# Loop one reordered: the next step's energies beside this step's transposed ones, last step's weighted values after them, then the whole products

## The chip, the cores and the metric

The kernel runs on one core of one Trainium2 chip. The metric is the time of one execution on the device in microseconds (us); less is better. Short names of the engines: PE is TensorE (matmuls), DVE is VectorE, ACT is ScalarE, POOL is GpSimd, SP issues most DMAs.

## The reference

Two layers run one after the other over `x` of 32 batches of 128 tokens by 512 features, each with a condition vector per batch. Only the first layer's loop is changed. Cut to that layer:

```python
h = gamma * layernorm(x) + beta                 # gamma, beta: one row per batch
q, k, v = split(h @ Wqkv.T + bqkv)              # 16 heads of 32 features
energy = einsum('bhqd,bhkd->bhqk', q, k)
att = softmax(energy, axis=-1) / D ** 0.5
out = einsum('bhqk,bhkd->bhqd', att, v) @ Wp.T + bp
h1 = out + x
x = gamma * layernorm(h1) + beta + h1           # same gamma, beta, weights
```

The second layer (one head, attention within a batch, a wide MLP with Gelu) follows; its kernel code is the same before and after.

## The kernel before, in words

**Loop one** is a Python loop over `STEPS` = 32 steps, unrolled. Batches are taken in groups of four (`G` = 4, eight groups); step `s` treats group `g = s // 4` and a quarter `c = s % 4` of the heads: four heads (r = 0 to 3, each 32 features, so 32 rows of the PE array) for four batches (i = 0 to 3).

The instructions of PE, DVE, ACT and POOL are issued in the order in which the code writes them (`tc.manual_schedule`); each of these queues works in that order, and waits on semaphores where data or a buffer is not ready. The order on SP is chosen by the scheduler, as are the buffers within a pool.

Parts of a step, by the names in the code:

- `qk0(s)`: two whole products (12 matmuls each, tiles `psq` and `psk`, three float32r partial products for each of four chunks); ACT adds the bias on the way out to `qk` (L548).
- `values0(b)`: one whole product of 12 matmuls (`psv`); ACT copies it out.
- `energies(s)`: q by k for four heads by four batches, with 32 rows of the array each (tiles `pse`, four banks; 32 matmul instructions); DVE takes the four maxima (`TENSOR_REDUCE`, L577) and writes `nmx`.
- `maxima(s)`: PE transposes `nmx` (`psm`). `spread_maxima(s)`: DVE spreads it into `mT` (L590).
- `exponentials(s)`: the energies transposed (`pst`, four banks), first a matmul by ones that puts in minus the maximum (L602), then k by q (L606), 32 rows each; ACT takes four exponentials (L613).
- `heads_out(s)`: the exponentials by the values (`pso`, L626) and their sums (`pss`, L631), both with 32 columns of the array for each head; ACT takes logarithm and `Exp` of its negative (L636, L637), DVE divides with three operations (L638 to L640), ACT and POOL split the result into `o..h` and `o..l`.
- `End(b)`, for a finished batch of the group before: `bias` (POOL, `xe` plus a row, L659), `stream` (the whole product `psp`, 12 matmuls), `add` (DVE, L674), `first` (statistics, DVE L688, POOL L689), `second` (DVE L693 and a store), `sums` (a load of `scw`), `third` (DVE L702).
- `Turned(layer, b)` prepares a batch: `stats`, `norm` (DVE), `halves` (ACT copy L422, then a transposing DMA), in the next step `merge` (DVE L431), `rest` (ACT) and `low` (DVE). In a step, `new` is the batch at the first half of this and `ready` the one at the second.
- `Weights.heads` and `Weights.tails`, in steps 4 to 23: ACT casts pieces of the second layer's MLP weights (`wmh`, L911), POOL subtracts (`wml`, L918) and forms sums of pieces (L921); five steps make a cycle, with one or two pieces and zero to two sums each.
- `extras`: single pieces of work in some steps (products `pswu`, `psrow`, `psc`, and `psvp` in the last four).

PSUM has eight banks: a pool `mm` of two (`mm_tile`), `s` of two (`s_tile`) and `e` of four (`e_bank`).

In step `s` the PE does, in order: `pse` of `s`, `psv`, `psq` of `s + 1`, seven matmuls of `psp`, `psm`, five more of `psp`, `pst` of `s`, `psk` of `s + 1`, `pso` and `pss` of `s`. The POOL does `rn`, End's `bias`, `re`, the add of L689, the weights' pieces and sums, and the low part of `o`. On ACT the weights' casts stand between the exponentials and the bias of `psk`.

Of the kernel before, what the change touches and what calls it, by code (L numbers as in the profile page):

```python
# [41 lines left out]
def cond_seq_kernel(ctx: ExitStack, tc, x, condT, wcond, w0, w1, wk1, wm1, wm2, cols, rows, out):  # L42
# [15 lines left out]
    def mm_tile(name):  # L58
        return ps_mm.tile([P, D], FP, tag="mm", name=name)

    def s_tile(name):
        return ps_s.tile([P, D], FP, tag="s", name=name)

    def e_bank(name):
        return ps_e.tile([P, D], FP, tag="e", name=name)
# [456 lines left out]
            row0, over_rows("psrow0", acc), ISD, bp, ALU.mult, ALU.add  # L522
        )

    def values0(b, by_part=False):
        g, i = divmod(b, G)
        hT = hs[0, g][0]

        def done(ps):
            if i == 0:  # L530
                vs[g] = w_tile(f"v{g}", FP)
            nc.scalar.copy(vs[g][:, i], ps)

        return mm3(
            lambda: mm_tile(f"psv{b}"),
            [(sub(hT, k, ts(i, P)), sub(W0["v"], k)) for k in range(KC)],
            done, by_part,
        )
# [54 lines left out]
        )  # L593
        mT[s] = t.rearrange("p i q -> p (i q)")

    def exponentials(s):

        banks = [e_bank(f"pst{s}_{r}") for r in range(4)]
        q, k = qk[s][:, 0], qk[s][:, 1]
        for r in range(4):  # L600
            rr = slice(32 * r, 32 * r + 32)
            nc.tensor.matmul(banks[r], over[rr], mT[s][rr], start=True, stop=False)  # L602
        for i in range(G):
            for r in range(4):
                rr = slice(32 * r, 32 * r + 32)
                nc.tensor.matmul(  # L606
                    banks[r][:, ts(i, P)], k[rr, ts(i, P)], q[rr, ts(i, P)],
                    start=False, stop=(i == G - 1),
                )
        es[s] = []  # L610
        for r in range(4):
            e = p_tile(f"e{s}_{r}")
            nc.scalar.activation(e, banks[r], AF.Exp)  # L613
            es[s].append(e)

    def heads_out(s):

        g, c = divmod(s, KC)
        e, v = es.pop(s), vs[g]
        if c == 0:  # L620
            os_[g] = w_pair(f"o{g}")
        pso, pss = s_tile(f"pso{s}"), s_tile(f"pss{s}")
        for i in range(G):
            for r in range(4):
                rr = slice(32 * r, 32 * r + 32)
                nc.tensor.matmul(  # L626
                    pso[rr, ts(i, P)], v[:, i, 32 * (4 * c + r) : 32 * (4 * c + r) + 32],
                    e[r][:, ts(i, P)], start=True, stop=True,
                )
        for r in range(4):  # L630
            nc.tensor.matmul(  # L631
                pss[32 * r : 32 * r + 32], rootd, e[r], start=True, stop=True
            )

        w = p_tile(f"rs{s}")
        nc.scalar.activation(w, pss, AF.Ln)  # L636
        nc.scalar.activation(w, w, AF.Exp, scale=-1.0)  # L637
        nc.vector.tensor_tensor(pss, pss, w, ALU.mult)  # L638
        nc.vector.tensor_tensor(w, pso, w, ALU.mult)
        nc.vector.scalar_tensor_tensor(w, pss, 2.0, w, ALU.subtract, ALU.mult, reverse0=True)  # L640
        hi, lo = (t[:, c] for t in os_[g])
        nc.scalar.copy(hi, w)
        nc.gpsimd.tensor_tensor(lo, w, hi.bitcast(FP), ALU.subtract)

    class End:
# [15 lines left out]
        def stream(self):  # L661
            g, i = divmod(self.b, G)

            def done(ps):
                self.ps = ps

            return mm3(
                lambda: mm_tile(f"psp{self.b}"),
                [(sub(os_[g], k, ts(i, P)), sub(W0["p"], k)) for k in range(KC)],
                done,  # L670
            )
# [516 lines left out]
    with tc.manual_schedule(engines=ordered):  # L1188
# [67 lines left out]
        for p in first:  # L1256
            p.stats()
            p.norm()
        run(values0(0, True))
        energies(0)  # L1260
        run(values0(1))
        first[0].rest()
        new = Turned(0, G + 2)
        new.stats()
        run(values0(2))
        cond_rows()
        maxima(0)
        spread_maxima(0)
        new.norm()
        new.halves()  # L1270
        run(values0(3))
        W0["p"] = w_pair("w0p")
        ready = first[1]

        def l1_chunk(j, c):
            return load(d_tile(f"w1c{j}_{c}", FP, (P, KC, P)), w1[:, j, :, ts(c, P)])
# [30 lines left out]

        def coming(s):

            if s + G + 2 < B:  # L1310
                return Turned(0, s + G + 2)
            return Turned(1, s - FIRST1) if s >= FIRST1 else None

        CQ = range(7, 15, 2)
        W_FIRST, W_STEPS = 4, len(Weights.TURNS)
        end = past = None
        staged = None
        for s in range(STEPS):
            q, k = qk0(s + 1) if s + 1 < STEPS else ([], [])
            if s:  # L1320
                energies(s)
            else:
                ready.rest()
                ready = None
            if ready:
                ready.merge()
            if 0 < s <= B - G:
                run(values0(s - 1 + G))
            if s >= STEPS - KC:
                staged()  # L1330
                staged = None
            run(q)
            projection = end.stream() if end else []

            ahead = 5 if s == STEPS - 1 else 7
            run(projection[:ahead])
            if s:
                maxima(s)
            if 0 < s < KC or s == STEPS - 1:
                spread_maxima(s)  # L1340
            if ready:
                ready.rest()
            if new and s:
                new.stats()
            if KC <= s < STEPS - 1:
                spread_maxima(s)
            if ready and s == STEPS - 1:
                ready.low(nc.vector)
            if new and s:
                new.norm()  # L1350
            if end:
                end.bias()
            if ready and s < STEPS - 1:
                ready.low()
            if end:
                run(projection[ahead:])
                end.add()
                end.first()
            elif staged:
                staged()  # L1360
                staged = None
            wn, wj = divmod(s - W_FIRST, W_STEPS)
            if s == KC:
                cond_features()
            if new and s:
                new.halves()
            exponentials(s)
            q2, late = divmod(s - W_FIRST, 3)
            if not late and 0 <= q2 < 4:
                nc.scalar.dma_start(out=w2d[q2], in_=wm2[:, q2])  # L1370
            if 0 <= wn < KC:
                weights.heads(wj)
                weights.tails(wj)
            if past:
                past.third()
                past = None
            if "cq" in L1:
                L1.pop("cq")()
            if end:
                end.second()  # L1380
                past = end
            if s == 0:
                staged = extras[0]()
            if s < KC:
                split_w(W0["p"], raw["p"], s, nc.gpsimd)
            coming_stage = extras[s + 1]() if s + 1 in extras else None
            run(k)
            if s == STEPS - 1:
                K = keys1(0)
                run(K[0])  # L1390
            heads_out(s)
            ready, new = new, coming(s + 1) if s + 1 < STEPS else None
            end = End(s + 1 - G, s + 1 == STEPS) if s + 1 >= G else None
            if past:
                past.sums()
            if s in CQ:
                L1["cq"] = l1_cq(CQ.index(s))
            if staged:
                staged()
            staged = coming_stage  # L1400
            if s == 2:
                later["mods"] = r_tile("mods")
            wn, wj = divmod(s + 1 - W_FIRST, W_STEPS)
            if 0 <= wn < KC and wj == 0:
                weights = Weights(wn)
            if s == STEPS - 2:
                l1_load()

        ends = [end]
        begins = {2 * b - 22: lambda b=b: Turned(1, b) for b in range(2 * G, B)}
        for b, slot in ((G + 1, -11), (G + 2, -10), (G + 3, -8)):
            begins[slot] = lambda b=b: Turned(1, b)
# [5 lines left out]
        for u, stream in enumerate(products):  # L1420
            pipe.start(u - 11)
            if u == 1:
                ready.merge()
            if isinstance(stream, int):
                e = ends[stream]
                e.bias()
                run(e.stream())
                e.add()
                e.put_off()
                if stream + 1 < G:  # L1430
                    ends.append(End((NG - 1) * G + stream + 1, True))
            else:
                run(stream)
            if u == 1:
                ready.rest()
                past.third()
            if u == 2:
                ready.low()
            pipe.end(u - 11)
# [153 lines left out]
```

## Time and profile before

| | before |
| --- | --- |
| time, median of 3 runs | 1455.6 us (1455.53 to 1456.17) |
| the profiled execution: its own time | 1455.66 us |
| its span | 1453.9 us, 24645 instructions |
| PE busy | 1441.2 us (99%) |
| DVE busy | 1032.8 us (71%) |
| ACT busy | 758.7 us (52%) |
| POOL busy | 434.9 us (30%) |
| chain that ended last, by engine | PE 88%, DVE 6%, ACT 2%, DMA 2%, POOL 1% |
| granted PE clock | 1.0 |

The span is one execution seen by the profiler; the profiled execution's own time is 1.8 us longer. A line of a timeline gives start and duration in us, engine, line of the kernel, operation, output and inputs, shapes and how many instructions are merged in it. Matmuls overlap in the pipeline, so the distance between starts tells more than a duration. Where an engine was idle before an instruction, the idle time and its releaser stand in brackets. Loop one's first `pse` starts at 34.9 us, and the first product after the loop's last heads starts at 553.5 us.

### The profile page before, as it was taken

The page shows a single profiled execution, that of the slowest core. Times are in us where ns is not written, and L with a number is a line of the kernel's source. Part 1 is how long each engine was busy: PE and PEld are TensorE (multiplying, and loading weights), DVE is VectorE, ACT ScalarE, POOL GpSimd, SP SyncE. Part 2 cuts the span into 40 slices and gives each one's busy share as a digit, 9 for nine tenths or more (in the row PEclk, how much of TensorE's full clock was granted, in tenths as well). Part 3 has the DMA queues.
Part 4 walks back from the last instruction along what each step waited for, and adds up shares of the span by engine and source line. Part 5 has one row for each costly group of instructions (what it writes and reads, how often), then busy time and mean ns, then how long its engine had stood idle before and what let it go on. Part 6 is the DMA issues. An engine that isn't in the chain of part 4 may idle for free.

```text
span 1453.9 us, 24645 instructions
## 1 busy us (share of the span) xinstructions
PE 1441.2 (99%) x9224; PEld 1142.8 (79%) x9224; DVE 1032.8 (71%) x1906; ACT 758.7 (52%) x1392; POOL 434.9 (30%) x396
## 2 busy tenths in 40 slices
PE   9999999999999999999999999999999999999998
PEld 5777777777777667887888888888888888888887
DVE  6668898988888788889987866755566655753442
ACT  4556656655665455677786454534453444523231
POOL 0125555464552334556560313100020002210000
PEclk9999999999999999999999999999999999999999
DMA  8446677947565355777798976846784676834450
GB/s 326 125 141 190 196 231 185 246 141 212 158 201 150 101 174 148 186 209 204 202 218 297 305 228 203 313 152 193 232 278 163 209 230 208 297 130 159 168 181 29
DMA packets 227871, 287.80 MB, mean 198 GB/s; under 512 B 107396, under 2 KB 138244, under 8 KB 226216
## 3 DMA queue, kind: packets, MB, share of 16 engines
q1 hardware_dynamic: 218240, 226.89, 52.6%
q10 hardware_dynamic: 9512, 59.34, 12.1%
q8 instruction: 72, 1.18, 0.3%
q14 instruction: 47, 0.39, 0.1%
HBM read 193.18 MB, written 73.60 MB: 183 GB/s over the span
## 4 chain that ended last, share of the span: by engine, by line
PE 88%; DVE 6%; ACT 2%; DMA 2%; POOL 1%; issue 1%; SPq 0%; POOLq 0%; ACTq 0%; DVEq 0%
PE acc L1044 24%; PE psh L164 21%; PE psp L164 6%; PE psk L164 6%; PE psv L164 5%; PE psq L164 5%; PE psT L164 4%; PE psV L164 4%; PE pso L626 2%; PE pse L565 2%; PE pss L631 2%; PE pst L606 2%; PE pss L809 1%; PE pso L164 1%; PE pst L602 1%; DVE nm L577 1%
## 5 line engine op out<-in xcount | busy, mean ns | idle before, releaser
L337 POOL TENSOR_TENSOR rn<-vn,neghalf 128x1 f32<-128x1 f32 x96 | 60.0, 625 | 510.2 <-DVE vn L335 372.8
L422 ACT COPY tn<-x 128x1024 uint16<-128x1024 uint16 x90 | 94.1, 1046 | 75.4 <-DVE x L408 61.1
L982 ACT ACTIVATE c<-c,col 128x512 f32<-128x512 f32 x64 | 46.4, 725 | 141.4 <-DVE c L1007 88.0
L1060 POOL TENSOR_TENSOR xe<-xe,row 128x512 f32<-128x512 f32 x32 | 45.2, 1443 | 202.3 <-DMA xe<-xs 156.4
L997 DVE TENSOR_TENSOR c<-psh,ca 128x512 f32<-128x512 f32 x32 | 22.1, 691 | 87.0 <-PE psh L164 83.4
L431 DVE COPY tn<-tn 128x1024 uint16<-128x1024 uint16 x90 | 79.1, 879 | 0.4 <-DMA tn<-tn 0.4
L577 DVE TENSOR_REDUCE nm<-pse 128x4 f32<-128x512 f32 x128 | 79.2, 681 | 0.0
L613 ACT ACTIVATE e<-pst 128x512 f32<-128x512 f32 x128 | 65.8, 600 | 1.8 <-PE pst L606 1.8
L325 DVE BATCH_NORM_STATS2 stn<-x 128x6 f32<-128x512 f32 x96 | 65.4, 681 | 1.9 <-DMA x<-in_x 1.8
L693 DVE SCALAR_TENSOR_TENSOR xe<-te,re,xe 128x512 f32<-128x512 f32 x28 | 40.9, 1462 | 28.6 <-POOL xe L689 28.6
L408 DVE TENSOR_SCALAR x<-x,rn 128x512 f32<-128x512 f32 x64 | 56.6, 884 | 6.2 <-POOL rn L337 5.4
L448 ACT ACTIVATE tn<-tn,mods 128x128 f32<-128x128 f32 x128 | 52.6, 483 | 14.0 <-DVE tn L431 14.0
L548 ACT ACTIVATE qk<-psq,col 128x512 f32<-128x512 f32 x32 | 22.1, 690 | 63.6 <-PE psq L164 62.6
L337 POOL TENSOR_TENSOR re<-ve,neghalf 128x1 f32<-128x1 f32 x32 | 30.8, 963 | 75.4 <-DVE ve L330 72.6
L565 PEld LDWEIGHTS pse<-qk 32*128 32x128 f32 x1024 | 32.0, 186 | 26.7 <-issue 18.4
L1010 DVE TENSOR_TENSOR ca<-psh,ca 128x512 f32<-128x512 f32 x32 | 22.1, 691 | 42.4 <-PE psh L164 42.4
L982 ACT ACTIVATE cb<-cb,col 128x512 f32<-128x512 f32 x32 | 23.2, 726 | 41.6 <-DVE cb L1011 41.6
L659 POOL TENSOR_TENSOR xe<-xe,row 128x512 f32<-128x512 f32 x32 | 42.2, 1317 | 2.3 <-DMA xe<-in_x 2.3
L638 DVE TENSOR_TENSOR pss<-pss,rs 128x512 f32<-128x512 f32 x32 | 22.3, 697 | 28.9 <-ACT rs L637 28.7
L448 ACT ACTIVATE tn<-tn,mod 128x128 f32<-128x128 f32 x104 | 42.6, 482 | 0.2 <-DVE tn L431 0.2
L1064 DVE TENSOR_TENSOR xe<-acc,xe 128x512 f32<-128x512 f32 x32 | 21.1, 688 | 30.3 <-PE acc L1044 30.3
L918 POOL TENSOR_TENSOR wml<-wm,wmh 128x512 fp32r<-128x512 f32 x28 | 40.8, 1468 | 0.0
(1388 smaller groups left out, 4741.7 us busy)
## 6 DMA issues: line engine op xcount, KB each, us to landing
mod<-mod SPq DMA_DIRECT2D x32, 512.0 KB, 5.9
x<-xs SPq DMA_DIRECT2D x64, 256.0 KB, 4.0
ur<-ud SPq DMA_DIRECT2D x64, 256.0 KB, 4.7
xs<-xe SPq DMA_DIRECT2D x60, 256.0 KB, 2.7
xe<-xs SPq DMA_DIRECT2D x60, 256.0 KB, 3.3
x<-in_x SPq DMA_DIRECT2D x32, 256.0 KB, 4.0
xe<-in_x SPq DMA_DIRECT2D x32, 256.0 KB, 3.9
scw<-scw SPq DMA_DIRECT2D x32, 256.0 KB, 4.9
```

Source lines behind the costliest of these rows:

```text
L164: nc.tensor.matmul(st["ps"], *calls[j], start=(j == 0), stop=(j == n - 1))
L325: nc.vector.bn_stats(st, t)
L337: nc.gpsimd.tensor_tensor(r, v, neghalf, ALU.pow)
L408: nc.vector.tensor_scalar(X, X, r, None, ALU.mult)
L422: nc.scalar.copy(halves.rearrange("p (e d) -> p e d", e=2), X.bitcast(U16).rearrange("p (d e) -> p e d", e=2),)
L431: nc.vector.tensor_copy(self.a.bitcast(U16).rearrange("p (f e) -> p e f", e=2), self.t.bitcast(U16).rearrange("p (e f) -> p e f", e=2),)
L448: nc.scalar.activation(dst[:, c], self.a[:, ts(c, P)], AF.Identity, bias=m[:, q + B : q + B + 1], scale=m[:, q : q + 1],)
L565: nc.tensor.matmul(banks[r][:, ts(i, P)], q[32 * r : 32 * r + 32, ts(i, P)], k[32 * r : 32 * r + 32, ts(i, P)], start=True, stop=True,)
L577: nc.vector.tensor_reduce(nm[:, r], chunks(banks[r]), AX.X, ALU.max, negate=True)
L613: nc.scalar.activation(e, banks[r], AF.Exp)
L982: nc.scalar.activation(t[nm], t[nm], AF.Gelu, bias=col[:, C_B1 + f : C_B1 + f + 1], scale=1.0)
L1044: nc.tensor.matmul(accs[i], u[pa][:, ts(i, P)], wb[f // 4][pb][:, f % 4, :], start=(first and j == 0), stop=(last and j == len(PARTS) - 1),)
```

## The change

The step is put in another order. Step `s` now begins with the energies of step `s + 1`, then the transposed energies of step `s` (`scores0`, split off from `exponentials`), then `heads_out` of step `s - 1`; after these come the whole products `psv`, (`psm` of `s + 1`), `psq` and `psk` of step `s + 2`, and `psp`, now in one piece. The three divisions and the split of the output are split off into `divided0`. `End.bias`, `stream` and `add` stand at the step's end, `first`, `sums`, `second` and `third` in the next step; an `End` object, and so its loads, is made within the step. The weights' casts stand after the bias of `psk` and after `halves`, and the weights' pieces and sums before `End.bias`. Batches are prepared one step earlier. What ran ahead of the loop now takes in `qk0(1)`; the last `heads_out` and division stand behind the loop.

The PSUM banks are dealt out anew: `pst` in two `mm` and two `s` banks (before four `e`), `pso` and `pss` in `e` (before `s`), `psv` in `e` (before `mm`), `psp` in `s` (before `mm`).

```diff
-    def exponentials(s):
+    def scores0(s):
-        banks = [e_bank(f"pst{s}_{r}") for r in range(4)]
+        banks = [(mm_tile if r < 2 else s_tile)(f"pst{s}_{r}") for r in range(4)]
...
-        es[s] = []
+        es[s] = banks
+
+    def exponentials(s):
+
         for r in range(4):
             e = p_tile(f"e{s}_{r}")
-            nc.scalar.activation(e, banks[r], AF.Exp)
-            es[s].append(e)
+            nc.scalar.activation(e, es[s][r], AF.Exp)
+            es[s][r] = e
...
-        pso, pss = s_tile(f"pso{s}"), s_tile(f"pss{s}")
+        pso, pss = e_bank(f"pso{s}"), e_bank(f"pss{s}")
...
+        es[s] = pso, pss, w
+
+    def divided0(s):
+
+        g, c = divmod(s, KC)
+        pso, pss, w = es.pop(s)
...
-                lambda: mm_tile(f"psp{self.b}"),
+                lambda: s_tile(f"psp{self.b}"),
```

The loop's body after the change, with the core of it in order:

```python
last = s == STEPS - 1
if not last:
    energies(s + 1)
scores0(s)
if s:
    heads_out(s - 1)
if ready:
    ready.merge()
exponentials(s)
if past:
    past.first()
    past.sums()
if s:
    divided0(s - 1)
if 0 < s <= B - G:
    run(values0(s - 1 + G))
if s >= STEPS - KC:
    staged()
    staged = None
if not last:
    maxima(s + 1)
if ready:
    ready.rest()
if last:
    ready.low(nc.vector)
if new:
    new.stats()
if not last:
    spread_maxima(s + 1)
end = End(s - G) if s >= G else None
q, k = qk0(s + 2) if s + 2 < STEPS else ([], [])
run(q)
if past:
    past.second()
if new:
    new.norm()
if ready and not last:
    ready.low()
run(k)
if s == KC:
    cond_features()
if new:
    new.halves()
...
if 0 <= wn < KC:
    weights.heads(wj)
    weights.tails(wj)
if past:
    past.third()
...
if end:
    end.bias()
    run(end.stream())
    end.add()
past = end
...
ready, new = new, None if last else coming(s + 1)
...
if staged:
    staged()
```

More of the change, by code (lines that the diff above doesn't have):

```diff
@@ L523, in l0_row, with values0 @@
         )
-    def values0(b, by_part=False):
+    def values0(b, by_part=False, make=None):
         g, i = divmod(b, G)
@@ L534, in values0 @@
         return mm3(
-            lambda: mm_tile(f"psv{b}"),
+            lambda: (make or e_bank)(f"psv{b}"),
             [(sub(hT, k, ts(i, P)), sub(W0["v"], k)) for k in range(KC)],
@@ L1258, in cond_seq_kernel @@
             p.norm()
-        run(values0(0, True))
+        run(values0(0, True, mm_tile))
         energies(0)
-        run(values0(1))
+        run(values0(1, make=mm_tile))
         first[0].rest()
@@ L1264, in cond_seq_kernel @@
         new.stats()
-        run(values0(2))
+        run(values0(2, make=mm_tile))
         cond_rows()
@@ L1270, in cond_seq_kernel @@
         new.halves()
-        run(values0(3))
+        q, k = qk0(1)
+        run(q)
+        first[1].rest()
+        run(k)
+        run(values0(3, make=mm_tile))
         W0["p"] = w_pair("w0p")
-        ready = first[1]
         def l1_chunk(j, c):
@@ L1308, in coming @@
         def coming(s):
-            if s + G + 2 < B:
-                return Turned(0, s + G + 2)
+            if s + G + 3 < B:
+                return Turned(0, s + G + 3)
             return Turned(1, s - FIRST1) if s >= FIRST1 else None
@@ L1315, in cond_seq_kernel @@
         W_FIRST, W_STEPS = 4, len(Weights.TURNS)
-        end = past = None
+        ready, new, end, past = new, coming(0), None, None
         staged = None
         for s in range(STEPS):
-            q, k = qk0(s + 1) if s + 1 < STEPS else ([], [])
+            last = s == STEPS - 1
+            if not last:
+                energies(s + 1)
+            scores0(s)
             if s:
[L1321 to L1324, printed above, removed]
+                heads_out(s - 1)
             if ready:
                 ready.merge()
+            exponentials(s)
+            if past:
+                past.first()
+                past.sums()
+            if s:
+                divided0(s - 1)
             if 0 < s <= B - G:
@@ L1331, in cond_seq_kernel @@
                 staged = None
[L1332 to L1340, printed above, removed]
+            if not last:
+                maxima(s + 1)
             if ready:
                 ready.rest()
-            if new and s:
+            if last:
+                ready.low(nc.vector)
+            if new:
                 new.stats()
[L1345 to L1349, printed above, removed]
+            if not last:
+                spread_maxima(s + 1)
+            end = End(s - G) if s >= G else None
+            q, k = qk0(s + 2) if s + 2 < STEPS else ([], [])
+            run(q)
+            if past:
+                past.second()
+            if new:
                 new.norm()
-            if end:
-                end.bias()
-            if ready and s < STEPS - 1:
+            if ready and not last:
                 ready.low()
[L1355 to L1362, printed above, removed]
+            run(k)
             if s == KC:
                 cond_features()
-            if new and s:
+            if new:
                 new.halves()
-            exponentials(s)
             q2, late = divmod(s - W_FIRST, 3)
@@ L1370, in cond_seq_kernel @@
                 nc.scalar.dma_start(out=w2d[q2], in_=wm2[:, q2])
+            wn, wj = divmod(s - W_FIRST, W_STEPS)
             if 0 <= wn < KC:
@@ L1375, in cond_seq_kernel @@
                 past.third()
-                past = None
             if "cq" in L1:
                 L1.pop("cq")()
-            if end:
-                end.second()
-                past = end
             if s == 0:
@@ L1386, in cond_seq_kernel @@
             coming_stage = extras[s + 1]() if s + 1 in extras else None
-            run(k)
-            if s == STEPS - 1:
+            if end:
+                end.bias()
+                run(end.stream())
+                end.add()
+            past = end
+            if last:
                 K = keys1(0)
                 run(K[0])
[L1391 to L1395, printed above, removed]
+            ready, new = new, None if last else coming(s + 1)
             if s in CQ:
@@ L1407, in cond_seq_kernel @@
                 l1_load()
-        ends = [end]
+        heads_out(STEPS - 1)
+        past.first()
+        past.sums()
+        divided0(STEPS - 1)
+        ends = [End((NG - 1) * G, True)]
         begins = {2 * b - 22: lambda b=b: Turned(1, b) for b in range(2 * G, B)}
@@ L1433, in cond_seq_kernel @@
                 run(stream)
+            if u == 0:
+                past.second()
             if u == 1:
```

## The prediction

> **What bounds the kernel now.** I read the page's busy line first, then the timeline of TensorE over one step of loop one (the 32 steps stand between 35 and 553 us), then the timelines of the other engines over the same step, and the order of the changed program's instructions with their waits.
>
> ```profile
> PE 1441.2 (99%) x9224; PEld 1142.8 (79%) x9224; DVE 1032.8 (71%) x1906; ACT 758.7 (52%) x1392; POOL 434.9 (30%) x396
> ```
>
> TensorE is the bound. In its timeline (start, duration, line, tile) one step reads:
>
> ```profile
> 302.05 0.40 PE L164 MATMUL psp<-w0ph,o3l 128*128 128x512 f32 x1
> ...
> 302.38 0.51 PE L602 MATMUL pst<-mT,over 32*128 32x512 f32 x4
> 302.71 1.06 PE L606 MATMUL pst<-qk 32*128 32x128 f32 x32
> 303.70 0.50 PE L164 MATMUL psk<-n_16h,w0kh 128*128 128x512 f32 x1
> 304.04 0.40 PE L164 MATMUL psk<-n_16l,w0kh 128*128 128x512 f32 x1
> ...
> 306.33 0.39 PE L164 MATMUL psk<-n_16h,w0kl 128*128 128x512 f32 x1
> 306.64 1.08 PE L626 MATMUL pso<-e,v 128*32 128x128 f32 x32
> 307.54 1.04 PE L631 MATMUL pss<-e,rootd 128*32 128x512 f32 x8
> 308.51 1.17 PE L565 MATMUL pse<-qk 32*128 32x128 f32 x32
> 309.62 0.50 PE L164 MATMUL psv<-w0vh,n_20h 128*128 128x512 f32 x1
> 309.95 0.39 PE L164 MATMUL psv<-w0vl,n_20h 128*128 128x512 f32 x1
> ```
>
> Whole matmuls start every 0.227 us; sets of four row-tiled ones every 0.112, column-tiled every 0.109. Wherever the tile shape changes, the next block starts about 0.1 late and its first set takes about 0.1 longer, its weight load standing bare. Step by step the energies (pse) of this kernel start exactly 15.79 us apart from step 5 to 26, with no other gap: nothing but matmuls and five changes of shape.
>
> The other engines in that step:
>
> ```profile
> 303.48 0.68 DVE L674 TENSOR_TENSOR xe<-psp,xe 128x512 f32<-128x512 f32 x1
> ...
> 312.01 2.48 DVE L577 TENSOR_REDUCE nm<-pse 128x4 f32<-128x512 f32 x4
> ```
>
> ```profile
> 302.99 1.05 ACT L422 COPY tn<-x 128x1024 uint16<-128x1024 uint16 x1 [0.50 <-DVE x L410]
> ...
> 305.87 0.64 ACT L911 CAST wmh<-wm 128x512 fp32r<-128x512 f32 x1
> 306.75 0.69 ACT L548 ACTIVATE qk<-psk,col 128x512 f32<-128x512 f32 x1 [0.24 <-PE psk L164]
> ```
>
> ```profile
> 301.38 1.29 POOL L659 TENSOR_TENSOR xe<-xe,row 128x512 f32<-128x512 f32 x1
> ...
> 307.66 1.26 POOL L918 TENSOR_TENSOR wml<-wm,wmh 128x512 fp32r<-128x512 f32 x1
> 308.89 3.11 POOL L921 TENSOR_TENSOR wm<-wm 128x512 f32<-128x512 f32 x2
> ```
>
> The reader is to see an order: End.bias (L659) runs on POOL before the weights' casts, and so the add (L674) follows psp at once; wmh is cast before k's bias.
>
> **What is saved.** By the single starts, a change into row tiles costs 0.21, out of them to whole 0.20 to 0.22, whole to column 0.115, column to row 0.21: 0.95 a step. The new step has row tiles (pse of s+1, then pst of s), column tiles, whole: three changes. Whole to row is 0.21; column to whole is not in the trace and lies between 0.20 and 0.22, its neighbours; row to column lies between 0.115 and 0.21, and I take 0.13, since the exposed load is the column one's (0.02). Work 14.77, changes 0.55, slow first spacings 0.04: 15.36 instead of 15.79, or 0.43 saved a step (0.35 with the dear end).
>
> **What is moved past what.** In the changed program POOL's order is: rn, the weights' lows (wml), their sums, and only then End.bias; ScalarE's order is k's bias, halves (L422), then wmh. So bias now stands at the end of a chain that starts with the last psk matmul. VectorE's add waits for bias. Behind the add stand the four maximum reductions, merge and everything else of the next step on VectorE; and the order with waits shows that the ones-matmul of pst bank 3 of the next step waits for that add, because psp now uses that bank (s_tile). TensorE is in order, so it stops there.
>
> Measured from the start K of the last psk matmul: k's bias starts at K+0.42 (306.33 to 306.75), the next ScalarE operation 0.60 later (q's bias and its follower: 299.62 to 300.21), after halves another 0.95 (302.99 to the exponentials at 303.94), the cast takes 0.64, the hand-over 0.05: the first wml starts at K+2.66. Each wml occupies POOL 1.24 (307.66 to 308.89). A sum takes 1.29 where VectorE is quiet and up to 1.74 beside its work (its own rows); VectorE is waiting here, so I take 1.27 apart. Then bias 1.29, add 0.68, two hand-overs: bias start plus 2.06. Without the wait the bank-3 matmul would start at K+0.23+2.72 (psp)+0.10+1.00 (pse) = K+4.04.
>
> The weights' work runs in steps 4 to 23 as a cycle of five, four times over: pieces (wml) and sums 2+0, 1+1, 1+2, 2+1, 1+0. Bank 3 is ready at K+7.20, 7.23, 8.50, 8.47, 5.96; stalls 3.16, 3.19, 4.46, 4.43, 1.92: 17.2 a cycle, 68.6 in all. With sums at 1.74 it is 76; below, the least rows give 67. Nothing hides it: the four reductions, merge, the exponentials and the divisions of the next step need the add or these matmuls first.
>
> SP: the load of xe is now issued in mid-step, but behind the preceding step's last wml store, some 14 us before bias needs it, against 3.9 us to land; mod (5.9 us), scw (4.9 us) and the transposes (3.2 us) land before their readers too. I cost them at nothing; if one fell late by 1 us in weights steps the same wait would cover it.
>
> The other steps, 24 to 27, gain 0.43 each. There bias follows rn directly and is done some 3 us before psp ends. The other new waits have little room: the add frees bank 3 about 0.15 before its use, and the first maximum frees pso's bank 0.34 before (energies' end, 0.68 of reduction), the third the values' bank 1 us before. Cost nothing, at worst half a microsecond a step.
>
> Start: step 0 has neither heads nor values between scores and maxima, so the transposed maxima wait for 2.8 us of reductions: 1.8 lost. The wu product at the step's end waits for VectorE's column sums, 0.9, and these hold the next reductions, 0.5; after cond_half(1), now last in step 3, five VectorE operations (3.5) stand before the reductions, 2.1. Together 5.3. Before had 1.9 of stalls there (0.97 in values after wu, 0.8 in pso, 0.15), and three and a half steps' changes save 1.5: net +1.9.
>
> End: in steps 29 to 31 psvp directly follows heads (no values left) and takes the bank that the first exponential frees; ScalarE does logarithm and reciprocal first, so TensorE waits pss end + 1.8 to 2. Before lost 0.5 there: with the saving +1.05 in 29 and 30. Step 28 gains 0.43; step 31 I count as even (no energies, but K of loop two late).
>
> **The sum**, against the profiled execution's 1455.66 (span 1453.9; the median of three runs is 1455.6, the same): steps 4 to 23 -8.6 +68.6, 24 to 28 -2.1, 29 to 31 +2.1, start +1.9: +62, or 1517.6.
>
> [...] The windows view at the kernel's end shows TensorE's last work (to 1449.97) and the granted clock:
>
> ```profile
> 1449.00:1450.00 1.00, 0.97 (x5) 0.47 (x3) 1.00 (x2) 0.00 (x0) 0.00 (x0) 1.00 0.38 145
> ...
> 1453.00:1454.00 1.00, 0.00 (x0) 0.00 (x0) 0.00 (x0) 0.00 (x0) 0.00 (x0) 0.73 0.00 0
> ```
>
> The clock falls to half at 1453.46, 3.5 us after. The first warm matmuls (256 columns) stand 0.427 apart, as far as 512 columns do from 6.3 us on: half speed for some 4.7 us of work. Idle stretches of 4.2 us come in eight steps of my sum; if each drops the clock for 4.7 us, TensorE loses 2.35 each, 19 in all; if none does, 0. I take 0, since one fall after 3.5 does not say that 4.2 suffices wherever it lies.
>
> [...]
>
> **Rivals.** *Late bias and the clock falls* in the eight long stalls: up to 1537. [...] *Late bias, but the changes of shape save nothing* (the load stays bare, another gap replaces it): 25 steps at 0.43 back, 1528. Against it: the gaps are the same in every step. *Faster:* bias is in time. Its place is POOL between rn and wml, the price of the stall is 0, and the rest leaves -6.7: 1449. It decides at K+2.95, psp's end: bias must be done by then. Since wmh is cast only after k's bias and halves, the first wml alone starts at K+2.66; only a POOL that does not work in order, or weights' steps that read little, would give that. The timelines show POOL in order.
>
> **Chances.** Late bias as summed 0.79, with the clock 0.10, without saving 0.05, faster 0.05, near no change 0.01. The likeliest is 1517.6. The range 1503 to 1537 takes in the terms' ends (stalls 67 to 76, start and end a few us either way, the hand-overs) and the clock case, and leaves out the faster one. What can be told from no change is 0.2%, 2.9 us: faster 0.05, same 0.01, slower 0.94.
>
> **What would show it.** Right: in steps 4 to 23 pse starts 17 to 20 us apart in a cycle of five, TensorE idle before L602's fourth matmul with VectorE's add as releaser, the add waiting for POOL's bias, and 15.36 in steps 24 to 27 with no gap between pse and pst. Wrong: steps of 15.4 throughout, bias done before psp's end, or waits that sit at pso (the maxima) or at psm instead.

## The result and the profile after

| | before | after |
| --- | --- | --- |
| time, median of 4 runs each | 1455.6 us (1455.0 to 1456.2) | 1565.8 us (1562.4 to 1567.6) |
| ratio to before, 95% interval | | 1.0754 [1.0733, 1.0776] |
| span of the profiled execution | 1453.9 us | 1565.4 us |
| mean granted clock of the span | 1.0 | 0.971 |
| first product after the loop's last heads | 553.5 us | 665.0 us |

The change costs 110 us, and in the traces all of it lies in loop one: the first product behind the loop starts 111.5 us later, the span is 111.5 us longer.

The page of the changed kernel: TensorE's busy line, the clock over forty slices of the span, and two groups (busy time and mean ns of one, then the idle time before them and who ended most of it).

```profile
PE 1476.4 (94%) x9224; PEld 1172.8 (75%) x9224; DVE 1009.4 (64%) x1906; ACT 753.6 (48%) x1392; POOL 429.2 (27%) x396
...
PEclk9999999899998999899999999999999999999999
...
L683 DVE TENSOR_TENSOR xe<-psp,xe 128x512 f32<-128x512 f32 x32 | 22.1, 690 | 128.1 <-POOL xe L668 120.7
...
L602 PE MATMUL pst<-mT,over 32*128 32x512 f32 x128 | 28.6, 492 | 67.0 <-DVE xe L683 66.0
```

The same 9224 matmuls fill 94% of a longer span, and they take 35 us longer in sum. The add (L683, 674 before) waits for POOL's bias (L668), and the ones-matmul L602 for the add. The list of TensorE's waits between 120 and 530 us has one line (total, times, longest):

```profile
PE pst L602 <- DVE xe L683: 62.2, 20, 4.7
```

One pause for each of the twenty steps with weights' work. The timeline of one of them:

```profile
473.96 0.69 ACT L548 ACTIVATE qk<-psk,col 128x512 f32<-128x512 f32 x1 [1.05 <-PE psk L164]
474.54 1.04 ACT L422 COPY tn<-x 128x1024 uint16<-128x1024 uint16 x1
475.48 0.62 ACT L920 CAST wmh<-wm 128x512 fp32r<-128x512 f32 x1
...
476.18 1.27 POOL L927 TENSOR_TENSOR wml<-wm,wmh 128x512 fp32r<-128x512 f32 x1 [4.22 <-ACT wmh L920]
...
477.41 2.60 POOL L930 TENSOR_TENSOR wm<-wm 128x512 f32<-128x512 f32 x2
477.48 0.49 PE L602 MATMUL pst<-mT,over 32*128 32x512 f32 x3
...
479.97 1.26 POOL L668 TENSOR_TENSOR xe<-xe,row 128x512 f32<-128x512 f32 x1
481.26 0.69 DVE L683 TENSOR_TENSOR xe<-psp,xe 128x512 f32<-128x512 f32 x1 [7.51 <-POOL xe L668]
...
482.01 0.79 PE L602 MATMUL pst<-mT,over 32*128 32x512 f32 x1 [4.04 <-DVE xe L683]
```

Read it downwards: k's bias, halves, cast, one piece, two sums, bias, add, and only then the fourth ones-matmul. Each line starts where the one before it ends; this is one chain over four engines. What the forecast left out stands in the windows view of the same place (length, then busy time and instructions of PE, PEld, DVE, ACT, POOL, then the granted clock):

```profile
477.90:481.30 3.40, 0.07 (x3) 0.00 (x0) 0.04 (x1) 0.00 (x0) 3.25 (x3) 1.00 0.99 275
481.30:484.70 3.40, 2.69 (x41) 2.45 (x45) 3.33 (x8) 0.00 (x0) 0.00 (x0) 0.55 0.12 45
484.70:488.10 3.40, 3.40 (x41) 1.62 (x33) 1.63 (x5) 0.00 (x0) 0.55 (x1) 0.50 0.02 5
```

After the pause the clock is at half for 6.8 us. In it sets of four matmuls of pso start 0.213 us apart (0.109 at full clock), whole matmuls 0.427 (0.227). Over loop one the records show 26 such stretches of 3.41 us, 88.8 us at half clock; TensorE was busy in 84.5 of them, so at about half speed it loses some 42. Twenty of the stretches stand behind 15 of the twenty pauses, one at the loop's start and five in its last three steps.

### The profile page after: what moved, and what is told of

It reads as the page before. It is cut to its first block, busy times and chain, and to the rows that moved or that the text cites. A ratio compares the mean times of both kernels' runs of the same rounds, so it can differ in the third digit from the quotient of the medians.

```text
span 1565.4 us, 24861 instructions
## 1 busy us (share of the span) xinstructions
PE 1476.4 (94%) x9224; PEld 1172.8 (75%) x9224; DVE 1009.4 (64%) x1906; ACT 753.6 (48%) x1392; POOL 429.2 (27%) x396
## 4 chain that ended last, share of the span: by engine, by line
PE 75%; DVE 8%; POOL 6%; issue 5%; ACT 3%; DMA 2%; SPq 0%; POOLq 0%; DVEq 0%; ACTq 0%
PE acc L1053 22%; PE psh L164 19%; PE psT L164 5%; PE psv L164 4%; PE psq L164 4%; PE psk L164 3%; PE psV L164 3%; PE pso L629 3%; PE pst L606 2%; POOL wml L927 2%; PE pss L634 2%; PE psp L164 2%; POOL xe L668 1%; POOL wm L930 1%; PE psvp L757 1%
## 5 line engine op out<-in xcount | busy, mean ns | idle before, releaser
L337 POOL TENSOR_TENSOR rn<-vn,neghalf 128x1 f32<-128x1 f32 x96 | 69.6, 725 | 449.9 <-DVE vn L335 367.8
L639 ACT ACTIVATE rs<-pss 128x512 f32<-128x512 f32 x32 | 19.2, 599 | 249.6 <-PE pss L634 249.6
L683 DVE TENSOR_TENSOR xe<-psp,xe 128x512 f32<-128x512 f32 x32 | 22.1, 690 | 128.1 <-POOL xe L668 120.7
L1069 POOL TENSOR_TENSOR xe<-xe,row 128x512 f32<-128x512 f32 x32 | 45.3, 1444 | 202.1 <-DMA xe<-xs 183.3
L602 PE MATMUL pst<-mT,over 32*128 32x512 f32 x128 | 28.6, 492 | 67.0 <-DVE xe L683 66.0
L431 DVE COPY tn<-tn 128x1024 uint16<-128x1024 uint16 x90 | 78.4, 871 | 11.2 <-DMA tn<-tn 8.8
L337 POOL TENSOR_TENSOR re<-ve,neghalf 128x1 f32<-128x1 f32 x32 | 24.1, 752 | 173.7 <-DVE ve L330 168.4
L602 PEld LDWEIGHTS pst<-mT,over 32*128 32x128 f32 x128 | 11.2, 190 | 74.3 <-DVE xe L683 72.6
L606 PE MATMUL pst<-qk 32*128 32x128 f32 x1024 | 52.0, 322 | 0.0
L629 PE MATMUL pso<-e,v 128*32 128x128 f32 x1024 | 47.7, 345 | 2.9 <-DVE nm L577 2.9
L606 PEld LDWEIGHTS pst<-qk 32*128 32x128 f32 x1024 | 46.7, 225 | 0.2
```

Source lines behind the costliest of these rows:

```text
L337: nc.gpsimd.tensor_tensor(r, v, neghalf, ALU.pow)
L431: nc.vector.tensor_copy(self.a.bitcast(U16).rearrange("p (f e) -> p e f", e=2), self.t.bitcast(U16).rearrange("p (e f) -> p e f", e=2),)
L606: nc.tensor.matmul(banks[r][:, ts(i, P)], k[rr, ts(i, P)], q[rr, ts(i, P)], start=False, stop=(i == G - 1),)
L629: nc.tensor.matmul(pso[rr, ts(i, P)], v[:, i, 32 * (4 * c + r) : 32 * (4 * c + r) + 32], e[r][:, ts(i, P)], start=True, stop=True,)
```

## The experiments

Theory: the late bias makes the pauses, and the pauses make the half clock. Rivals: the new order itself slows TensorE; or the clock falls for some other reason than idle time.

**1. The bias early.** One step of the code is moved:

```diff
             wn, wj = divmod(s - W_FIRST, W_STEPS)
+            if end:
+                end.bias()
             if 0 <= wn < KC:
                 weights.heads(wj)
                 weights.tails(wj)
...
             if end:
-                end.bias()
                 run(end.stream())
```

> The changed kernel with one edit: End.bias (POOL) stands before the weights' casts, pieces and sums instead of after them. Late-bias theory (the add waits for bias, bank 3 of the transposed energies waits for the add, and the idle stretches make the clock fall): in steps 4 to 23 pse starts 15.4 us apart as in steps 25 and 26 of the changed kernel (15.35), no half clock between 130 and 510 us, the time 1565.8 - 62 (waits there) - 36 (slow clock there) - 3, so 1455 to 1470, of which about 10 are lost in steps 0 and 29 to 31. Rival, the new deal of the PSUM banks (psp in an s bank, the add frees it too late whenever bias is done): the waits of L602 for the add stay above 1 us a step, the time stays over 1500.

Measured: 1475.7 us, ratio 1.0137 [1.0114, 1.016], mean clock 0.988. TensorE's waits between 120 and 530 us:

```profile
PE pst L602 <- DVE xe L683: 4.8, 3, 2.9
PE pse L565 <- DVE x L410: 2.7, 2, 2.2
PE psvp L757 <- ACT e L616: 1.9, 1, 1.9
```

Of 62.2 us 4.8 are left; 90 of the 110 us come back by the place of one POOL instruction. Most distances between energies are now 15.35 (I number them: the nth goes from `pse` of n to `pse` of n + 1 and holds loop step n - 1; the expectations from here on count steps so, but for the loop's last ones). The time is still some 6 us above what I expected: numbers 9 to 16 hold one of 20.4 and one of 21.5 us and lose about 15 in all, taken up in 6 to 8. (Each stands behind a transposing DMA that went out at once, 0.03 us after `halves`, but took 7.8 and 8.8 us to land, against a median of 4.2.)

**2. The casts before the keys instead.** `weights.heads` and `weights.tails` in front of `run(k)`, the bias left at the end.

> The changed kernel with the weights' casts, pieces and sums moved before the product k and its bias on ScalarE; End.bias stays behind them on POOL. Late-bias theory: the chain to the add begins one product (2.7 us) and halves (0.95) earlier, so steps with 2+0, 1+1 and 1+0 pieces and sums have no wait, those with 1+2 and 2+1 about 0.8 us; no long idle stretch, no slow clock in steps 5 to 24; time 1465 to 1478. Rival (bias waits for something else, such as the load of xe, or VectorE is late by itself): waits as before the edit, time over 1540.

Measured: 1534.2 us, ratio 1.0539 [1.0505, 1.0573]. A miss by some 60 us. TensorE's and VectorE's waits in the same stretch:

```profile
PE pst L602 <- DVE xe L683: 31.2, 16, 3.5
PE pse L565 <- ACT qk L548: 9.0, 4, 3.3
```

```profile
DVE tn L431 <- DMA tn<-tn: 30.9, 13, 5.1
```

Half of the old wait is left, and a new one has come. The timeline of SP at one of these steps:

```profile
301.34 0.49 SPq L934 DMA_DIRECT2D ad<-wml  x1
301.93 4.11 SPq L426 DMA_TRANSPOSE tn<-tn  x1
```

The transposing DMA now comes behind the store of wml, which I had not counted, but that is the smaller part: `halves` ends at 301.60, so it goes out 0.33 us later here and 1.0 in the median (0.03 in the changed kernel). It also takes longer to land, a median of 6.2 us instead of 3.1; why, no run separates. The merge (L431) of the next step waits for it (5.1 us at most), and VectorE's divisions, ScalarE's splits and casts and then k's bias, which the next energies need, are late behind it.

**3. The pauses filled.** Useless matmuls in each pause, into banks that the real ones overwrite:

```diff
+        for _ in range((11, 11, 17, 17, 6)[s % 5] if 5 <= s <= 24 else 0):
+            for r in range(3):
+                rr = slice(32 * r, 32 * r + 32)
+                nc.tensor.matmul(banks[r], over[rr], mT[s][rr], start=True, stop=True)
         for r in range(4):
```

> The changed kernel with useless matmuls by ones into banks 0 to 2 of the transposed energies ahead of the real ones, in steps 5 to 24: 6, 11 or 17 sets of three, sized to fill most of the wait for bank 3 (1.4 to 3.9 us); their results are overwritten. Theory that the half clock after idle stretches costs 36 us there: the chain through POOL is as long as before, the clock stays full in steps 5 to 24, and the kernel is faster with more work: 1526 to 1534. Rival (the steps over 17 to 18.5 us come from longer POOL or ScalarE work, not from the clock): no gain, 1560 to 1575.

Measured: 1537.1 us, ratio 1.056 [1.0528, 1.0591]: more work, and 28.6 us faster than the changed kernel. The windows view from 130 to 235 us, of the changed kernel and then of this one:

```profile
130.00:235.00 105.00, 87.70 (x804) 67.03 (x808) 62.45 (x125) 46.98 (x87) 42.24 (x38) 0.92 0.59 164
```

```profile
130.00:235.00 105.00, 103.41 (x1096) 80.43 (x1091) 68.33 (x138) 50.34 (x94) 47.34 (x40) 1.00 0.61 173
```

The fourth ones-matmul still starts only when the add has ended, and the clock does not fall here. In the twenty filled steps it falls once, at 326.2 us, behind 2.8 us of a longer pause that the fill left open (number 16, 22.9 us). So the half clock comes from idle time and not from the order or from load. The other steps, now free of it, measure the pauses: 18.6, 18.8, 20.0, 19.85, 17.3 us (one of 17.75), that is 3.3, 3.4, 4.6, 4.5 and 2.0 above 15.35. The forecast had 3.16, 3.19, 4.46, 4.43, 1.92.

**4. Only the sums behind the bias.** `Weights.tails` split in two: the pieces stay where they are, the sums follow `end.bias()`.

> The changed kernel with only the sums of the weights' pieces (0, 1, 2, 1, 0 in the five steps of a cycle) moved behind End.bias on POOL; the pieces stay ahead of it. Late-bias theory: waits fall by 1.27 us for each sum, to 3.2, 1.9, 1.9, 3.2, 1.9 us by the cycle, 12.1 instead of 17.2: 20 us less waiting, and the clock falls in fewer steps; 1525 to 1545. Rival (only the first cast counts, the queue behind it does not): no change, 1560 to 1570.

Measured: 1527.5 us, ratio 1.0493 [1.0462, 1.0524], TensorE's wait 41.9 us. Steps with one piece take 17.3 to 17.4 whatever sums they have, steps with two pieces 20.15 to 20.2, of which 1.7 is for a half-clock stretch (number 16: 23.05). What POOL does ahead of the bias is paid for nearly in full, as the sum had it.

**5. The pauses half filled.** As 3, with `(5, 5, 8, 8, 3)`.

> The changed kernel with useless matmuls in about half of each pause of TensorE in steps 5 to 24 (they write banks that the real ones then overwrite); the waits stay as they are and the idle time that is left in a pause is 1.0 to 2.1 us instead of 1.9 to 4.5. Theory that the clock falls after a 3.41 us stretch of the grid in which TensorE worked less than about half: nearly all of the 34 us come back, 1531 to 1541 (a few stretches with 2.1 us idle still fall). Rival, that any pause of over 1 us is followed by a stretch at half clock: 1555 to 1566. Rival, that only a wholly idle stretch of 3.41 us counts: the clock is full in all of steps 5 to 24, 1530 to 1533; but then the pauses of under 3.2 us in the changed kernel should not have cost anything either.

Measured: 1560.4 us, ratio 1.0728 [1.0707, 1.075]. My theory's number missed: the steps with the longer pauses take 20.25 to 22.9 as without fill, but for 18.75 and 19.9 in numbers 17 and 18 (number 16: 23.5). What is left of the pauses, 1.6 to 2.2 us (3.5 in number 16), still drops the clock except in these two; the shortest pauses, 0.8 us, don't. The windows view on the grid of 3.413 us on which the clock changes in the changed kernel's trace (see the last section), here:

```profile
189.71:193.12 3.41, 1.92 (x27) 1.24 (x21) 0.13 (x1) 0.00 (x0) 3.25 (x3) 1.00 1.17 166
193.12:196.53 3.41, 2.79 (x41) 2.55 (x45) 3.34 (x8) 0.00 (x0) 0.00 (x0) 0.50 1.13 358
```

and in the changed kernel, around a pause of 2.9 us that a boundary of the grid cuts into 1.3 and 1.5:

```profile
355.32:358.73 3.41, 2.09 (x39) 1.38 (x37) 0.00 (x0) 0.22 (x1) 2.98 (x3) 1.00 0.72 157
358.73:362.15 3.42, 1.87 (x53) 1.75 (x57) 2.62 (x5) 0.00 (x0) 0.77 (x1) 1.00 0.71 231
362.15:365.56 3.41, 3.41 (x37) 2.23 (x30) 3.27 (x9) 1.87 (x4) 0.81 (x1) 1.00 0.15 52
```

and there again, around a pause of 2.8 us that lies within one stretch:

```profile
437.24:440.66 3.42, 0.66 (x15) 0.45 (x16) 1.19 (x2) 0.00 (x0) 2.19 (x2) 1.00 0.97 252
440.66:444.07 3.41, 3.41 (x66) 3.05 (x62) 3.34 (x8) 0.00 (x0) 0.00 (x0) 0.50 0.76 231
```

In the half-filled run 1.5 us idle in one stretch brought half clock. In the changed kernel 2.8 us in one stretch did, and 2.9 us across a boundary cost nothing. The time lies where the first rival had it, but its rule does not hold either, since the pause of 2.9 us and pauses of 1.5 us in the changed kernel cost nothing; and the second rival falls, for no wholly idle stretch is needed. What decides in these traces is how much of one stretch is idle. About half is the border and not a sharp one: with 1.92 us busy the clock fell, with 1.87 it did not.

**6 to 8. What was left with the early bias.** I put the 15 us of numbers 9 to 16 down to `l1_cq`, which in steps 7, 9, 11 and 13 loads two rows through SP. First they were moved (`CQ = range(22, 26)`):

> The bias early, as in the run before it (1475.7 us), and the four pieces of layer one's query row (l1_cq, two small loads each at the end of a step) moved from steps 7, 9, 11, 13 to steps 22 to 25. Theory: in steps 8 to 16 of the run with the early bias about 15 us were lost (steps of 20.4 and 21.5 us among steps of 15.35) because those loads wait on SyncE's queue for a buffer (up to 7.1 us) and the next load of x and the transposing DMA stand behind them, so that GpSimd's rn (5.2 us) and VectorE's merge (4.5 us) come late. Then the steps go to 15.35 and the time to 1460 to 1464; the steps 23 to 26, which have little work on GpSimd, lose under 3 us. Rival: the loss comes from the weights' stores in those steps; then the time stays at 1474 to 1478.

Measured: 1471.3 us, ratio 1.0116 [1.0096, 1.0136]. Distances 6 to 14 go to 15.35, about 2 us stay in 15 and 16, but 25 to 28 lose 9: the trouble moves with the loads, and the time misses the 1460 to 1464 expected. With three more waits mended:

> As the run with the early bias and the later query row, and three more waits of the changed kernel taken away: the value weights of layer one in steps 29 to 31 in a bank of the energies' pool instead of one that waits for the first exponential (1.9 us each), the VectorE row of step 4 that follows the conditioning's second half (2.9 us) put into the middle of the step, and VectorE's weighted sum behind the addition in the last two steps (3.8 us). Theory: 3 + 3 x 1.9 + 3.8 us and the half clock that follows them, some 3.5 us: 1445 to 1452, faster than the kernel before (1455.6). Rival: another wait in steps 29 to 31 comes last in their place: 1455 to 1462.

Measured: 1467.1 us, ratio 1.0083 [1.0061, 1.0106]. Number 30 fell from 19.7 to 16.0, but VectorE's row, moved into the middle of step 4, gained 3 us in number 5 and lost 6.4 in 6 and 7. A miss. Then the loads on ScalarE's queue, in their old steps, to see whether it is SP's order:

> As the run with the early bias, and: the two loads of layer one's query row stay in steps 7, 9, 11, 13 but go out on ScalarE's queue, which runs behind the work that frees their buffers, instead of SyncE's; the value weights of layer one in steps 29 to 31 in a bank that doesn't wait for the first exponential; the conditioning's second half ahead of the keys of step 3; VectorE's weighted sum behind the addition in the last two steps. Theory: the 15 us of steps 9 to 16 come back (the queue is what holds the merges), 3.7 us in step 29, 2 to 3 us in step 4, some 4 us in steps 30 and 31: 1475.7 less 20 to 25, so 1451 to 1456. Rival: ScalarE's queue holds the halves instead (0.4 to 0.8 us of issue in front of the keys' bias), or the merges wait still: 1460 to 1472.

Measured: 1473.5 us, ratio 1.0132 [1.0112, 1.0152]: numbers 9 to 16 still lose 20 us. The theory of the queue falls: between 130 and 430 us the transposing DMAs go out 0.03 us after `halves`, so nothing on SP holds them, but two land only 8.1 and 11.6 us later, and the merges wait. Two of SP's waits between 160 and 310 us in this run:

```profile
SPq L86 <- POOL o2l L652: 13.9, 2, 8.3
SPq L86 <- POOL o3l L652: 9.0, 1, 9.0
```

Its loads (L86) wait, with the rows gone from SP, for POOL's last read of a buffer of the pool of eight that exponentials, divisions and rows share. In runs 6 and 7, with the rows in later steps, SP has no such wait there. So two more buffers taken in a step look like the cost, whoever issues the loads; how that makes the transfers land late is not shown. The companion run, with the rows late and the queries of step 0 moved up:

> As the run before it, but the query row's loads on SyncE's queue and in steps 22 to 25, as in the run that moved them, where steps 25 to 28 then lost 9 us; and the queries of step 0 ahead of its maxima (a wait of 1.9 us and the half clock after it). Theory: 1471.3 less 3.7, 2 to 3, 4 and 2: 1457 to 1461. Rival: step 0 waits for the first exponential instead, and nothing comes back there: 1460 to 1464.

Measured: 1463.0 us, ratio 1.0063 [1.0048, 1.0078]; loop step 0 lost 3 us instead of gaining (15.4 instead of 12.4; `pswu` waited 4.6 us for VectorE), and the time lies where the rival had it, for another reason than the rival's.

**9 and 10. A version that beats both.** The rows in a tile of another pool, and the end of the loop rearranged:

```diff
-        w, bq = load(p_tile(f"wk{c}"), wk1[:, c]), row_of(R_BQ1)
+        w, bq = load(w_tile("wq", FP), wk1), row_of(R_BQ1, make=l_tile)
...
-        banks = [(mm_tile if r < 2 else s_tile)(f"pst{s}_{r}") for r in range(4)]
+        pools = [mm_tile, mm_tile, s_tile, e_bank if s == STEPS - 1 else s_tile]
+        banks = [pools[r](f"pst{s}_{r}") for r in range(4)]
...
+            if s == STEPS - 2:
+                maxima(s + 1)
+                spread_maxima(s + 1)
             if past:
                 past.first()
```

> All that helped so far in one kernel: the bias early; layer one's query row from one tile of another pool, loaded in step 23 and used in steps 24 to 27, so that no step takes two more of the eight buffers that the exponentials share; the value weights of layer one not behind the first exponential; the conditioning's second half ahead of the keys of step 3; and for the last two steps the maxima of step 31 ahead of the other work of VectorE in step 30, the next piece of weights loaded earlier, and the last bank of step 31's transposed energies from the energies' pool, so that it doesn't wait for the addition. Theory: every step from 5 to 27 at 15.35 but for some 2 to 3 us around step 15 (1455 without the change at the end, from 1473.5 less 18), and 4 to 8 us less in steps 30 and 31, where the run before it waited 3.8 us for the maxima and 3.0 us for the addition, with half clock after both: 1447 to 1452, faster than the kernel before. Rival: the end waits for the heads of the last block instead: 1453 to 1457, no faster than before.

Measured: 1456.4 us, ratio 1.0009 [0.9999, 1.0018]; numbers 9 to 16 lose 3.4 us in all instead of 15, much as with the late rows in the old pool (2.2 in run 6, 3.6 in the companion run). What the other pool adds shows in 25 to 28, which lose 1.1 us instead of 9.0 and 6.3 there. The rows also come in two loads instead of eight here, so pool and number of loads are not told apart. The rival held at the end; TensorE's longest wait from 500 to 600 us:

```profile
PE psT L164 <- ACT n_0h L457: 7.2, 1, 7.2
```

The last block's heads were the next thing late, so the first four blocks of layer one were turned a step earlier (`FIRST1 = STEPS - G - 2`; none is begun in step 30):

> As the run before it, with the first four blocks of layer one turned one step earlier (steps 26 to 29 instead of 27 to 30), so that the first whole product after the loop doesn't wait for the last block's heads. In the run before it that wait was 7.2 us, and a stretch of 3.4 us at half clock followed. Theory: the wait goes, and the half clock with it: 1456.4 less 7 to 9, so 1447 to 1450, faster than the kernel before by 0.3 to 0.5%. Rival: the turning in steps 26 to 29 collides there with the query row and the weights' loads (each step 1 to 2 us longer): 1451 to 1456.

Measured: 1449.0 us, ratio 0.9952 [0.9938, 0.9965], the fastest version. From its page:

```profile
PE 1431.0 (99%) x9224; PEld 1146.4 (79%) x9224; DVE 1022.3 (71%) x1905; ACT 752.6 (52%) x1392; POOL 434.8 (30%) x397
...
PEclk9999999999999999999999999999999999999999
```

TensorE's busy time is 10 us below that of before (1441.2); 0.43 a step over some 24 steps is as much. That fits the gain in time, 7 us, being the change's own saving less what still waits, though the edits at the loop's end have their share in it.

## Why the prediction was wrong

- **The mechanism held.** Bias behind the weights' work, add behind bias, bank 3 behind add: the waits and the timeline show each link, and run 1 takes it away.
- **The saving held.** Loop steps 25 and 26 take 15.35, forecast 15.36; so three changes of shape instead of five are worth 0.44 a step (15.79 before). The rival without saving is out.
- **The stalls held.** Steps with one piece and no sum took 17.31 to 17.35, forecast 17.28; the others are within 0.25 us by run 3, where the clock is full. (A sum took 1.26 in the changed kernel, with VectorE idle, and 1.29 to 1.74 beside VectorE's work in the kernel before; the 1.29 rows of before had VectorE busy for 95% and more.) Only number 16 has a pause 1.9 us longer than its kind (4.7 us). One step earlier a transposing DMA took 8.6 us to land, where the forecast took 3.2 and a cost of nothing, and the merge waited 2.0 us for it; that the one made the other is likely, not tried by itself.
- **The clock is the term that failed.** I had taken it as 0 and priced it at 19 at most. Measured some 42 us (26 stretches), 33 of them behind the weights' pauses and the rest at the loop's start and end, behind waits that the sum had priced by their length alone. The step that went wrong was to read the one fall in the trace of before, after 3.5 us of idle time, as the least idle time that brings a fall. It was the only case there, an upper bound (TensorE was idle for the whole 3.41 us ahead of that fall, 1450.05 to 1453.46); the lower one was not in that trace, and the range should have reached to a fall in all twenty stalls. Gaps under 3 us counted too: a pause of 2.8 us brought 3.41 us of half clock, as did pauses of 1.6 us in run 5.
- **Start, end.** The waits at the start come to 5.3 us as forecast, in other parts (2.9, 1.9, 0.5), with a half-clock stretch at 58 us behind one; steps 25 and 26 as forecast; step 31, counted as even, waited 3.8 us for the add and ran partly at half clock.
- Sum for the profiled execution: 62 forecast, 42 clock, 3.8 step 31, 1.9 number 16, the last 1.9 unexplained: 111.6 (1567.25 less 1455.66).
- **The faster rival** named 1449 as the value without the stall. Moving the bias alone gave 1475.7: other waits were hidden by the stall and came out once it was gone. With those mended as well it was 1449.0. That the two figures agree is partly luck: the last runs also removed waits at the loop's end that the rival had kept in its sum, and still lose 3.8 us in numbers 15 and 16.

## What to carry to other kernels

When a step is moved to the end of a loop body, list for each in-order queue what now stands in front of it, and follow the buffers of what it feeds: one 1.3 us operation held a PSUM bank, and with it TensorE, in twenty steps. A pause of TensorE had two prices here, its length (62.2 us in the twenty steps) and the half clock after it (some 33 us there), so put a price on the second even where the trace of before shows hardly any fall. Taking a stall away shows the waits that it hid; expect a part of the gain to go there, and look at shared buffer pools and at how long a transfer takes to land before blaming a queue.

## What the runs showed of the hardware

- In the changed kernel's trace the granted clock changes 42 times from 10.58 to 1563.64 us, each time a whole number of 3.413 us after the time before (1, 2, 5, 10, 14, 21, 30 and 266 of them); in the kernel before the two changes, at 6.21 and 1453.46 us, stand 424 of them apart. By TensorE's busy time in such stretches from 30 to 1556 us: the 20 at full clock in which it was busy for 1.65 us or less were all followed by half clock, the 401 others, with 1.87 us or more, by full clock. In the half-filled run one with 1.92 us was followed by half clock. Of the 26 at half clock, the six in which TensorE was busy for 1.55 to 3.18 us were followed by another, the 20 in which it was busy throughout by full clock.
- Half clock lasted one stretch (3.41 us) after 14 of these 20 falls and two (6.83 us) after six; at about half speed that is up to 1.7 or 3.4 us of TensorE's work for a fall.
- The falls kept step with the loop: three of the four weights' cycles of the changed kernel take 102.1 to 102.2 us (one 103.7), and 30 stretches are 102.4, so a pause fell in nearly the same place of the grid one cycle later. That fits that nearly every long one counted; it was not tried by itself.
